# Gated recurrence and binarized FFN: half of chunk 10's gates ahead of the loop, the recurrence step ahead of up group 0, and chunk 14's low part ahead of a shift and an addition

## The chip, the cores and the metric

The kernel runs on one core of a Trainium2 chip. The metric is the device time of one execution in microseconds; lower is better. Five engines work side by side, each through its own queue of instructions: PE (matrix products), DVE and ACT (elementwise work), POOL (elementwise work) and SP, which here only issues transfers.

## The reference

Two layers run over x of shape 2 x 4096 x 256 (batch, time, features). The first is a gated recurrence with a state of 64:

```python
u = x @ W_in + b_in
g = sigmoid(x @ W_gate + b_gate)
h_t = tanh(h_prev @ A + u_t @ Bm)
y_t = h_t @ C.T + u_t @ D.T
y_t = g_t * y_t + (1.0 - g_t) * x_t
r = ys @ W_out + b_out + x
x1 = layernorm(x + r)
```

The second is a feed-forward layer with a width of 1024, whose weights are their signs times the mean magnitude of each row:

```python
h = gelu(x1 @ bw1.T + b1)
out = layernorm(x1 + h @ bw2.T + b2)
```

All is float32.

## The kernel before, in words

**Recurrence.** Each sequence is cut into 64 segments that run side by side, so one step of the recurrence handles 2 x 64 columns. There are 64 steps, preceded by 48 warm-up steps from which the states at the segments' beginnings come: 112 in all. A step (`steps`, L156) is one matmul on PE (L157) and one tanh on ACT (L158), and it reads the tanh of the step before it. Function `step` (L673) puts one into the order if its inputs are there and steps are left; `emit` (L664) does the same by a count of PE's cost in the part ahead of the loop.

**Chunks.** The 64 time positions are handled as 16 chunks of 4 positions, 512 columns each. For one chunk the work is:

- gates: four matmuls (two halves `m`, two parts `k`) and a tanh for each half (`gates`, L300, written as a generator that yields after so many blocks of 128 columns)
- `mix` (L369) and `mix_end` (L384): C and D times state and input, then the gated sum on DVE
- `project` (L392): the product with W_out in blocks, then a sum on DVE
- `stats1`, `shift`, `norm`: the first layer norm; statistics on DVE, the power -0.5 on POOL (L265), the shift on DVE (L270), the application on ACT (L278)
- a transposed copy of the normalized block, split into a high part `xhi` on ACT and a low part `xlo` on DVE. For chunks 0, 1 and 15 `turn` (L425) does this through PE; for the others `blocks` (L444) transposes 32 x 32 squares on DVE and sends 16 small transfers through SP's queue into `xlo`, then `split_hi` (L461) copies `xlo` to `xhi` on ACT and `split_lo` (L466) subtracts on DVE
- `rest` (L472): b2 added on POOL
- `up` in four groups of eight matmuls (L486), each followed by two gelus (L496) and a cast (L505) on ACT; `low` (L508) subtracts the cast from the gelus on DVE
- `down` in four groups of 16 matmuls (L528)
- `add`, `stats`, `store`: the scaled sum, the second layer norm (shift and application in `store`, L559) and the transfer out

**Order.** The program order of each engine is written out by hand (`manual_schedule`, L697); no scheduler changes it. Ahead of the loop, the gates of chunks 0 to 9 are handed out by `parts` (L693) three blocks at a time between the steps. The loop over c (L777) then interleaves four chunks: up and down of chunk c, down groups 2 and 3 and the store of c - 1, the layer norm and split of c + 1, mix and project of c + 2, and two gate matmul pairs of chunks 10 to 15 from L814. In one iteration with 0 < c < 14 PE's order is: up 0 (L784), step, down 2 of c - 1, mix, up 1, step, down 3 of c - 1, gates, up 2, step, down 0, project, up 3, step, down 1. ACT's order beside it, from up 2 on, is: two gelus, cast, tanh of the step, `split_hi`, four applications of the store of c - 1 (L832), two gelus of up 3, cast, tanh of the step, four applications of `norm` of chunk c + 2, two gelus of up 0 of c + 1.

**Buffers.** The gates, the inputs' product and the up groups share three PSUM banks (`p_1`, L63); the step has one (L149). The transposed x has eight buffers (XTB), the gates nine (TGB).

Of the kernel before, what the change touches and what calls it, by code (L numbers as in the profile page):

```python
# [18 lines left out]
KD = DM // P  # L19
# [7 lines left out]
NC = L // SPC  # L27
TB = N // P
# [9 lines left out]
def gated_recurrence_then_binary_ffn(  # L38
# [16 lines left out]
    nc = tc.nc  # L55
# [68 lines left out]
    def u_of_chunks(*chunks):  # L124

        n = N * len(chunks) // 2
        parts = [(chunks[0], 0), (chunks[1], 0) if len(chunks) == 2 else (chunks[0], 1)]
        ps = p_1.tile([P, N], FP, tag="h", name=f"ps_u{chunks[0]}")
        for k in range(KD):
            for (c, i), r in zip(parts, (LOW, TOP)):  # L130
                nc.tensor.matmul(  # L131
                    ps[r, :n],
                    w_in[k],
                    x_tiles[c][:, k, bass.ts(i, n)],
                    start=k == 0,
                    stop=k == KD - 1,
                    skip_group_check=True,
                )
        for (c, i), r in zip(parts, (LOW, TOP)):
            to = u_of[:, bass.ds(c * SPC + i * n // W, n // W)].rearrange("p j b k -> p (j b k)")  # L140
            if r is TOP and c == FIRST:
                nc.scalar.activation(to, ps[r, :n], AF.Identity, bias=bin_c[r, :])
            else:
                nc.vector.tensor_scalar(to, ps[r, :n], bin_c[r, :], None, ALU.add)
        have_u.update(chunks)
        yield
# [144 lines left out]
    def later(what, *args):  # L291
        if waiting is None:
            what(*args)
        else:
            waiting.append((what, args))
            if len(waiting) > 1 and not held:
                what, args = waiting.pop(0)
                what(*args)

    def gates(chunks, size, x_of=lambda c: x_tiles[c.c]):  # L300

        room = size
        for c in chunks:
            xt_ = x_of(c)
            c.t = wk.tile([P, KD, N], FP, tag="tg", name=f"tg{c.nm}", bufs=TGB)
            for m in range(KD):
                ps = p_1.tile([P, N], FP, tag="h", name=f"ps_g{c.nm}_{m}")
                for k in range(KD):
                    i = 0
                    while i < TB:  # L310
                        n = min(room, TB - i)
                        cut = bass.ds(i * P, n * P)
                        nc.tensor.matmul(  # L313
                            ps[:, cut],
                            w_gate[:, k, bass.ts(m, P)],
                            xt_[:, k, cut],
                            start=k == 0 and i == 0,
                            stop=k == KD - 1,
                            skip_group_check=True,
                        )  # L320
                        i += n
                        room -= n
                        if k == KD - 1 and i == TB:
                            later(c.tanh, m, ps)
                        if room == 0:
                            room = size
                            yield

    class Chunk:

# [28 lines left out]
                nc.gpsimd.tensor_tensor(r[:, i, :], r[:, i, :], row, ALU.add)  # L359

        def gate(self):
            yield from gates([self], TB, lambda c: c.xt)

        def tanh(self, m, ps):
            nc.scalar.activation(
# [193 lines left out]
        def store(self, blocks=range(TB), engine=nc.vector, queue=nc.sync):  # L559

            cut = slice(blocks[0], blocks[-1] + 1)
            if engine is nc.scalar:
                self.st2.shift(blocks)
            self.st2.apply(blocks, engine)
            queue.dma_start(
                out=self.at(out, self.c)[:, cut, :], in_=self.x1[:, cut, :]
            )
            yield
# [69 lines left out]
    ch = [Chunk(c, f"{c}") for c in range(NC)]  # L638
# [8 lines left out]
    def ready():  # L647
        return done < len(plan) and plan[done] // SPC in have_u

    def next_steps():  # L650
        nonlocal done
        steps(plan[done])
        done += 1
        if done == WARM:
            first_states()
        for i in range(3):
            if done == WARM + (i + 1) * SPC:
                ch[i].load_h()
        if waiting and not held:
            for what, args in waiting:  # L660
                what(*args)
            waiting.clear()

    def emit(what, pieces, pace=5600):  # L664
        nonlocal since
        for _ in pieces:
            since += COST.get(what, 0)
            if since >= pace:
                since = min(since - pace, pace // 2)
                if ready():  # L670
                    next_steps()

    def step():  # L673
        if ready():
            next_steps()

    def do(i, what, *args, pace=5600):
        if not 0 <= i < len(ch):
            return
        if what == "load":  # L680
            need = WARM + (ch[i].c + 1) * SPC
            while done < need:
                next_steps()
            ch[i].load_u()
            ch[i].load_h()
        elif what in ("load_n", "load_x", "load_gate_x"):
            getattr(ch[i], what)()
        else:
            emit(what, getattr(ch[i], what)(*args), pace)

    early = gates([ch[i] for i in (4, 5, 6, 7, 0, 1, 2, 3, 8, 9)], 3)

    def parts(n, pace):  # L693
        emit("part", (next(early, None) for _ in range(n)), pace)

    ET = mybir.EngineType
    with tc.manual_schedule(engines={ET.PE, ET.Activation, ET.DVE, ET.Pool, ET.SP}):  # L697
# [39 lines left out]
        for i in range(4):  # L737
            ch[i].xt = x_tiles[i]
        ch[0].in_x = ch[1].in_x = True
        parts(1, 600)  # L740
        do(0, "mix", pace=850)
        do(0, "mix_end")
# [13 lines left out]
        do(0, "norm")  # L756
        do(1, "project", 1, pace=1700)
        do(1, "stats1")
        parts(1, 1700)
        while waiting:  # L760
            next_steps()
        waiting = None
# [4 lines left out]
        do(1, "norm", nc.vector)  # L767
        do(0, "rest")
        next(mixed)
        parts(2, 1700)  # L770
        for i in (4, 5):
            do(i, "load_x")
        end = len(ch) - 1
        parts_met = compare()
        since = -1 << 40
        late = gates(ch[10:], TB)
        for c in range(end):  # L777
            far = 0 < c < end - 1
            if far:
                do(c + 1, "shift")  # L780
                do(c + 1, "norm")
                do(c - 1, "low", 3)
                do(c + 1, "blocks")
            do(c, "up", 0)  # L784
            if c == end - 1:
                do(c - 1, "low", 3)
                do(c + 1, "shift")
                do(c + 1, "norm")
            step()
            do(c - 1, "down", 2)  # L790
            if c > 0:
                do(c + 2, "mix")
            do(c, "low", 0)
            mixed = ch[c + 2].mix_end() if 0 < c < end - 1 else iter(())
            next(mixed, None)
            if c == end - 1:
                assert done == len(plan), done
                next(parts_met)
                next(parts_met)
            do(c + 3, "load")  # L800
            do(c + 6, "load_x")
            if c % 2 == 0:
                do(10 + c // 2, "load_gate_x")
            do(c, "up", 1)
            step()
            do(c - 1, "down", 3)
            next(mixed, None)

            if c <= 12 or c == end - 1:
                do(c - 1, "add")  # L810
            if c <= 12:
                do(c - 1, "stats")
            if 1 <= c <= 12:
                emit("gate", (next(late, None) for _ in range(KD)))  # L814
            if not far:
                do(c + 1, "turn")
            do(c, "low", 1)
            if c == end - 2:
                do(c - 1, "add")
            if c > 12:  # L820
                do(c - 1, "stats")
            if c == end - 1:
                next(parts_met)
                next(parts_met)
            do(c + 1, "rest")
            do(c, "up", 2)
            step()
            if far:
                do(c + 1, "split_hi")
            do(c, "low", 2)  # L830
            if c < end - 1:
                do(c - 1, "store", range(TB), nc.scalar)  # L832
            do(c + 3, "load_n")
            do(c, "down", 0)
            do(c + 2, "project", 0)
            if c == end - 2:
                do(c + 1, "split_lo")
            do(c + 2, "project", 1)
            if far and c < end - 2:
                do(c + 1, "split_lo")  # L840
            do(c + 2, "stats1")
            do(c, "up", 3)
            if c == end - 1:
                do(c - 1, "store", range(TB), nc.scalar)
            step()
            do(c, "down", 1)
# [82 lines left out]
```

## Time and profile before

| what | value |
|---|---|
| median of 3 runs | 438.04 us (437.59 to 438.13) |
| the profiled execution's own time | 437.67 us |
| its span | 435.9 us |
| mean granted PE clock | 0.994 |
| PE busy | 425.5 us (98%) |
| DVE busy | 332.4 us (76%) |
| ACT busy | 286.0 us (66%) |
| POOL busy | 155.8 us (36%) |
| traffic | 51.34 MB, mean 118 GB/s |

The span is from the first instruction to the last of one profiled execution; what lies around it, 1.8 us here, is part of the time. A group's row in the profile gives source line, engine, operation, the tile written and those read, shapes and count, then busy time, the mean of one in ns, and the idle time of that engine just ahead of it with what ended it. A timeline row gives start and duration in us. A matmul instruction of float32 data shows as two records. Matmuls overlap each other in the records, so their pace is read from start to start.

### The profile page before, as it was taken

To read this page: it belongs to the slowest core of one execution; us is meant where nothing else is said; L and a number is where in the kernel's file an instruction comes from. 1 tells how busy PE (TensorE), PEld (TensorE's weight loads), DVE (VectorE), ACT (ScalarE), POOL (GpSimd) and SP (SyncE) were. 2 spreads that over 40 slices of the span, in tenths; PEclk is the share of its full clock that TensorE was granted. 3 is DMA by queue.
4 is the path that set the end of the run, shared out by engine and by line. 5 is a ranking of instruction groups with operands and counts; after the bars stand their busy time and mean duration, and the time that the engine had idled before them with its cause. 6 is when DMAs were issued, how large, how long until landed. Compare 5 with 4: busy or idle time off the path is not lost.

```text
span 435.9 us, 6818 instructions
## 1 busy us (share of the span) xinstructions
PE 425.5 (98%) x2402; PEld 344.3 (79%) x2402; DVE 332.4 (76%) x569; ACT 286.0 (66%) x480; POOL 155.8 (36%) x176
## 2 busy tenths in 40 slices
PE   8999999999999999999999999999999999999992
PEld 5665767788888879797979797978888888888982
DVE  0245937895979798888888897979797979797674
ACT  2443452486587776767677776777767585849881
POOL 1000050474143435253525443444343444533413
PEclk9999999999999999999999999999999999999997
DMA  8877713400251615152426242534233232311102
GB/s 297 300 282 261 269 36 128 163 2 0 44 174 44 217 46 178 38 186 80 144 66 192 76 144 69 166 102 124 91 107 109 58 111 60 111 36 50 48 2 102
DMA packets 31479, 51.34 MB, mean 118 GB/s; under 512 B 5328, under 2 KB 19664, under 8 KB 31440
## 3 DMA queue, kind: packets, MB, share of 16 engines
q1 hardware_dynamic: 30864, 50.48, 36.4%
q8 instruction: 21, 0.34, 0.3%
q10 hardware_dynamic: 576, 0.37, 0.3%
q14 instruction: 18, 0.15, 0.1%
HBM read 31.43 MB, written 8.39 MB: 91 GB/s over the span
## 4 chain that ended last, share of the span: by engine, by line
PE 89%; DVE 5%; ACT 2%; DMA 1%; issue 1%; POOL 1%; SPq 0%; POOLq 0%; DVEq 0%
PE ps_h L486 25%; PE ps_o L528 25%; PE ps_g L313 12%; PE ps_z L399 11%; PE ps_y L374 6%; PE ps_s L157 6%; PE ps_u L131 3%; DMA xt<-in_xT 1%; DVE hlo L512 1%; ACT xn L278 1%; POOL rs_b L265 1%; PE ps_t L430 1%; DVE bs_b L255 1%; DVE d L381 1%; ACT h L496 1%
## 5 line engine op out<-in xcount | busy, mean ns | idle before, releaser
L528 PE MATMUL ps_o<-sg,hhi 128*128 128x256 f32 x496 | 121.4, 286 | 0.0
L528 PE MATMUL ps_o<-sg,hlo 128*128 128x256 f32 x496 | 117.9, 279 | 0.1
L496 ACT ACTIVATE h<-ps_h,bias_c,al 128x512 f32<-128x512 f32 x128 | 95.5, 771 | 16.8 <-PE ps_h L486 13.0
L528 PEld LDWEIGHTS ps_o<-sg,hhi 128*128 128x128 f32 x496 | 93.5, 189 | 1.1 <-DVE o L544 0.3
L528 PEld LDWEIGHTS ps_o<-sg,hlo 128*128 128x128 f32 x496 | 93.5, 188 | 1.1 <-DVE hlo L512 0.3
L486 PE MATMUL ps_h<-xhi,sg 128*128 128x512 f32 x256 | 92.9, 444 | 0.3 <-ACT h L496 0.3
L359 POOL TENSOR_TENSOR xn<-xn,bo_r 128x256 f32<-128x256 f32 x64 | 54.7, 888 | 88.6 <-DMA xn<-in_x 78.4
L512 DVE TENSOR_TENSOR hlo<-h,hhi 128x1024 fp32r<-128x1024 f32 (+1 forms) x65 | 79.5, 1240 | 5.0 <-ACT hhi L505 5.0
L486 PE MATMUL ps_h<-xlo,sg 128*128 128x512 f32 x256 | 80.1, 394 | 0.2
L265 POOL TENSOR_TENSOR rs_b<-rs_b,neg_half 128x4 f32<-128x4 f32 (+1 forms) x17 | 28.1, 1655 | 115.1 <-DVE rs_b L264 105.0
L505 ACT CAST hhi<-h 128x1024 fp32r<-128x1024 f32 (+1 forms) x65 | 67.4, 1039 | 2.0
L313 PE MATMUL ps_g<-xt,w_gate 128*128 128x384 f32 (+3 forms) x208 | 66.2, 430 | 0.1
L486 PEld LDWEIGHTS ps_h<-xhi,sg 128*128 128x128 f32 x256 | 46.5, 189 | 18.9 <-issue 11.7
L158 ACT ACTIVATE st<-ps_s 64x128 f32<-64x128 f32 x112 | 30.0, 268 | 45.7 <-PE ps_s L157 45.3
L486 PEld LDWEIGHTS ps_h<-xlo,sg 128*128 128x128 f32 x256 | 48.0, 188 | 11.9 <-DVE xlo L440 0.7
L157 PEld LDWEIGHTS ps_s<-st,wab 128*128 128x128 f32 x224 | 38.5, 189 | 21.6 <-ACT st L158 9.7
L359 POOL TENSOR_TENSOR xn<-xn,b_r 128x256 f32<-128x256 f32 x64 | 52.9, 855 | 1.1 <-PE ps_t L430 1.1
L399 PE MATMUL ps_z<-w_out,tg 128*128 128x256 f32 x224 | 50.6, 379 | 0.0
L399 PEld LDWEIGHTS ps_z<-w_out,tg 128*128 128x128 f32 x224 | 41.4, 190 | 5.1
L157 PE MATMUL ps_s<-st,wab 128*128 128x128 f32 x224 | 43.8, 277 | 0.1
L278 ACT ACTIVATE xn<-xn,nm_a,rs_a 128x256 f32<-128x256 f32 x60 | 31.2, 591 | 14.4 <-DVE nm_a L270 14.3
L265 POOL TENSOR_TENSOR rs_a<-rs_a,neg_half 128x4 f32<-128x4 f32 x16 | 17.2, 1072 | 65.0 <-DVE rs_a L264 63.0
(79 smaller groups left out, 481.5 us busy)
## 6 DMA issues: line engine op xcount, KB each, us to landing
xt<-in_xT SPq DMA_DIRECT2D x35, 512.0 KB, 4.4
xn<-in_x SPq DMA_DIRECT2D x16, 512.0 KB, 3.4
out_y<-xn SPq DMA_DIRECT2D x15, 512.0 KB, 2.6
xlo<-xb SPq DMA_DIRECT2D x208, 32.0 KB, 1.9
hu<-st SPq DMA_DIRECT2D x32, 128.0 KB, 2.3
w1t<-in_w1T SPq DMA_DIRECT2D x2, 512.0 KB, 4.9
w1n<-in_w SPq DMA_DIRECT2D x2, 512.0 KB, 6.1
w2t<-in_w2T SPq DMA_DIRECT2D x2, 512.0 KB, 5.2
```

The source lines that it names most:

```text
L157: nc.tensor.matmul(p_h, ab, st[:, j].rearrange("p b k -> p (b k)"), start=True, stop=True)
L158: nc.scalar.activation(h_of[:, j + 1].rearrange("p b k -> p (b k)"), p_h[TOP, :], AF.Tanh)
L265: nc.gpsimd.tensor_tensor(rs, rs, neg_half[:, cut], ALU.pow)
L278: nc.scalar.activation(r, r, AF.Identity, bias=self.sh[:, i : i + 1], scale=rs)
L313: nc.tensor.matmul(ps[:, cut], w_gate[:, k, bass.ts(m, P)], xt_[:, k, cut], start=k == 0 and i == 0, stop=k == KD - 1, skip_group_check=True,)
L359: nc.gpsimd.tensor_tensor(r[:, i, :], r[:, i, :], row, ALU.add)
L399: nc.tensor.matmul(self.ps_z[:, i, :], self.y[:, k, bass.ts(i, P)], w_out[:, k, :], start=k == 0, stop=k == KD - 1,)
L486: nc.tensor.matmul(ps, sg1[:, k, bass.ts(j, P)], part[:, k, :], start=n == 0, stop=n == 2 * KD - 1,)
L496: nc.scalar.activation(to, ps.rearrange("p (a i c) -> p a i c", a=P // 32, c=32) if self.far else ps, AF.Gelu, bias=b1_c[:, j : j + 1], sc ...
L505: nc.scalar.copy(hi[:, part, :], h[:, part, :])
L512: nc.vector.tensor_sub(lo[:, i, :], h[:, i, :], hi[:, i, :].bitcast(FP))
L528: nc.tensor.matmul(ps[:, i, :], part[:, j % 2, bass.ts(tb, P)], sg2[:, j, :], start=j == 0 and part is self.h[j // 2][0] and first, stop=j ...
```

## The change

Four edits are made; the computation stays what it was.

- The gate generators for chunks 4 to 9 and 0 to 3 and for chunks 10 to 15 become one stream, whose piece size is 3 blocks ahead of the loop and 4 from the loop on. Ahead of the loop, `parts` takes one piece more ahead of chunk 0's turn and one more ahead of the loop: that is the first half of chunk 10's gates. Iteration 1 takes no gates any more. Chunk 10's x is loaded ahead of chunk 0's mix, not in iteration 0.
- For c > 0 the step that followed up group 0 comes ahead of it, right after down group 1 of the iteration before.
- In iteration 13 `split_lo` of chunk 14 is followed by the shift of chunk 12's store, which so far came ahead of it; the store's four applications and its transfer come after up group 3.
- In iteration 13 `rest` of chunk 14 comes after `stats1` of chunk 15, ahead of up group 3, no longer ahead of up group 2.

```diff
     def gates(chunks, size, x_of=lambda c: x_tiles[c.c]):
 
-        room = size
+        room = size[0]
         for c in chunks:
...
                         if room == 0:
-                            room = size
                             yield
+                            room = size[0]
...
-            yield from gates([self], TB, lambda c: c.xt)
+            yield from gates([self], [TB], lambda c: c.xt)
...
-            if engine is nc.scalar:
+            if engine is nc.scalar and not hasattr(self.st2, "sh"):
                 self.st2.shift(blocks)
...
-    early = gates([ch[i] for i in (4, 5, 6, 7, 0, 1, 2, 3, 8, 9)], 3)
+    size = [3]
+    stream = gates([ch[i] for i in (4, 5, 6, 7, 0, 1, 2, 3, 8, 9, *range(10, NC))], size)
 
     def parts(n, pace):
-        emit("part", (next(early, None) for _ in range(n)), pace)
+        emit("part", (next(stream) for _ in range(n)), pace)
...
         ch[0].in_x = ch[1].in_x = True
+        do(10, "load_gate_x")
         parts(1, 600)
...
-        parts(1, 1700)
+        parts(2, 1700)
         while waiting:
             next_steps()
...
-        parts(2, 1700)
+        parts(3, 1700)
...
-        late = gates(ch[10:], TB)
+        size[0] = TB
         for c in range(end):
...
+            if c > 0:
+                step()
             do(c, "up", 0)
...
-            step()
+            if c == 0:
+                step()
             do(c - 1, "down", 2)
...
-            if c % 2 == 0:
+            if c > 0 and c % 2 == 0:
                 do(10 + c // 2, "load_gate_x")
...
-            if 1 <= c <= 12:
-                emit("gate", (next(late, None) for _ in range(KD)))
+            if 2 <= c <= 12:
+                emit("gate", (next(stream) for _ in range(KD)))
...
-            do(c + 1, "rest")
+            if c != end - 2:
+                do(c + 1, "rest")
...
-            if c < end - 1:
+            if c < end - 2:
                 do(c - 1, "store", range(TB), nc.scalar)
...
                 do(c + 1, "split_lo")
+                ch[c - 1].st2.shift(range(TB))
...
             do(c + 2, "stats1")
+            if c == end - 2:
+                do(c + 1, "rest")
             do(c, "up", 3)
-            if c == end - 1:
+            if c >= end - 2:
                 do(c - 1, "store", range(TB), nc.scalar)
```

## The prediction

> **What bounds the kernel now.** I read the page's busy shares first, then the waits by total, then the chain of waits, then the timelines of PE and ACT around the places that the diff touches. The first line says that PE is the bound; the two lines from the table of waits are the longest that PE itself has in the whole span.
>
> ```profile
> PE 425.5 (98%) x2402; PEld 344.3 (79%) x2402; DVE 332.4 (76%) x569; ACT 286.0 (66%) x480; POOL 155.8 (36%) x176
> PE ps_s L154 <- POOL ones L107: 1.0, 1, 1.0
> PE ps_h L486 <- ACT h L496: 0.3, 1, 0.3
> ```
>
> Since a waiting matmul can be drawn as a long one, I checked starts against starts: 16 down matmuls take 1.83 us, 8 up matmuls 1.83 us, a recurrence step 0.22 us, four gate records 1.72 us, and one loop iteration 22.51 us (up group 0 at 215.76, then 238.27). That is the sum of its matmuls. The loop has almost nothing to give; it can only get worse. Lost time lies in three places: about 1.3 us between 83 and 91 us, 0.92 us at 391.85, and the start and end, which the diff leaves alone.
>
> Next, what a step needs. A step's matmul reads the tanh of the step before. This is ACT's timeline near the end of one iteration (start, duration):
>
> ```profile
> 230.83 0.26 ACT L158 ACTIVATE st<-ps_s 64x128 f32<-64x128 f32 x1
> 234.15 1.05 ACT L463 CAST xhi<-xlo 128x1024 fp32r<-128x1024 f32 x1 [3.06 <-DVE nm_b L270]
> 235.10 2.08 ACT L278 ACTIVATE xn<-xn,nm_b,rs_b 128x256 f32<-128x256 f32 x4
> 237.08 1.43 ACT L496 ACTIVATE h<-ps_h,bias_c,al 128x512 f32<-128x512 f32 x2
> 238.54 1.05 ACT L505 CAST hhi<-h 128x1024 fp32r<-128x1024 f32 x1
> 239.50 0.27 ACT L158 ACTIVATE st<-ps_s 64x128 f32<-64x128 f32 x1
> 240.12 2.08 ACT L278 ACTIVATE xn<-xn,nm_a,rs_a 128x256 f32<-128x256 f32 x4 [0.36 <-DVE nm_a L270]
> ```
>
> And PE's timeline over the same stretch:
>
> ```profile
> 236.22 0.38 PE L157 MATMUL ps_s<-st,wab 128*128 128x128 f32 x2
> 236.35 0.37 PE L528 MATMUL ps_o<-sg,hhi 128*128 128x256 f32 x1
> ...
> 238.15 0.28 PE L528 MATMUL ps_o<-sg,hlo 128*128 128x256 f32 x1
> 238.27 0.62 PE L486 MATMUL ps_h<-xhi,sg 128*128 128x512 f32 x2
> ```
>
> The step after up group 3 is multiplied at 236.22, but its tanh stands on ACT behind the copy xhi, four applies, two gelus and a cast, and ends at 239.77. PE is at up group 0 at 238.27. Today nobody cares, because the next step comes only after that group, at 240.10. The xhi copy is late because of the small transfers into xlo:
>
> ```profile
> ACT xhi L463 <- DMA xlo<-xb: 17.7, 7, 2.9
> ```
>
> What PE does when it meets such a tanh is seen once, ahead of chunk 0's turn: up group 1 would end at 90.52, and the step starts at 90.74, 0.06 after the tanh (90.42 + 0.26).
>
> ```profile
> 90.06 0.62 PE L486 MATMUL ps_h<-xlo,sg 128*128 128x512 f32 x2
> 90.74 0.49 PE L157 MATMUL ps_s<-st,wab 128*128 128x128 f32 x2
> ```
>
> **What the Trainium skill says.** "TensorE: Matmul & The Clock Gate", section "Step-by-step: what each phase is for": only weight loads are pulled ahead, matmuls stay in program order. The trace agrees: nothing overtook the step at 90.74. So work behind a waiting step waits too. The same page, "Back-to-back issue gap", gives N/2.4 + 2.5 ns warm, 216 ns for 512 columns; the up group's pitch here is 228 ns, so no faster matmul is hidden under these groups. "Perfetto Trace Analysis", section "Identifying the Most-Contended Engine", warns that matmul busy time says little on headroom, hence the start-to-start sums. "DMA: Bandwidth & Descriptors", section "Latency and other measured facts", puts a fixed cost of about 2 us on a transfer; the page here shows 1.9 us for xlo to land, after 16 issues on SP's queue at some 0.64 us each.
>
> **The change, part by part.**
>
> *Gates ahead of the loop.* Two more parts stand before the loop: chunk 10's first gate half, eight blocks in four pieces, 8 x 0.215 = 1.72 us of PE (before: two 512-column matmuls, the same streaming). One more part stands ahead of chunk 0's turn, one more ahead of its up group 0. Two stalls there are filled. The fourth normalized block ends at 83.88, and turn, begun at 83.25, took 1.28 instead of 0.80 us; with 0.65 us more ahead of it, it begins at 83.90 and loses perhaps 0.05. Up group 0 started near 86.05 and got its second xlo half late:
>
> ```profile
> 86.59 1.10 PE L486 MATMUL ps_h<-xlo,sg 128*128 128x512 f32 x2
> 87.52 0.63 PE L486 MATMUL ps_h<-xhi,sg 128*128 128x512 f32 x2
> ```
>
> That cost 0.55 us. In the new order it starts at 82.60 + 1.30 + 0.85 (turn) + 0.44 (mean of w2) + 1.30 (two parts) + 0.22 (step) + 0.64 = 87.35, with both xlo halves done near 87.3. It ends at 89.18 against 88.46: +0.72, of 1.72 us moved. 1.00 us is gained. The stall at 90.74 stays as it is. The extra tanh (0.69 us) falls where ACT idles. The transfer of chunk 10's x goes ahead of two hu loads on SP, which is idle from 63.68 to 67.25; at 4.4 us it lands by 69, needed at 85. The loads of x for chunks 5 and 6 now take buffers of chunks 0 and 1, free at 76.5 and 82.4; behind them hu and xn of chunk 3 slip to about 84, needed after 103. Nothing.
> In iteration 1 the 1.72 us of gates disappear from PE.
>
> *Step ahead of up group 0*, ten times (chunks 1 to 10). Its 0.22 us only changes places. The price is the new wait. The tanh ended after up group 0's old start by 0.18, 1.33, 1.17, 1.04, 0.84, 0.58, 1.50, 0.88, 1.29 and 0.40 us in the ten iterations; each wait would be that plus 0.06. Behind the waiting step stand the up group, down 2, mix and all the rest. But a wait also slackens the next: the tanh hangs on transfers that began with the project of the iteration before, which ends ahead of the wait. Two equations follow. With z the start of project and S of the step: next z = S + 15.16 (238.27 to 253.42, 215.76 to 230.91). S is the later of z + 7.35 and the tanh's end + 0.06. The tanh's end is the last iteration's norm + 15.1 to 16.5 us (to the xhi copy, by iteration) + 5.6. That norm is at its z + 9.2 to 9.6, or behind its own tanh. Lower bound of the wait: even with ACT free, a tanh ends 2.23 us after its up group (200.74 to 202.97) and the down takes 2.05, so 0.24.
>
> Carried through: iteration 0 ends with S at 103.23 + 0.72 + 0.24 = 104.19. Iteration 1's project is at 104.19 + 15.16 - 1.72 = 117.63, but its tanh hangs on the norm at 105.26: xhi at 122.17, tanh 127.78, so PE, ready at 124.98, waits 2.9 us. The missing gates are eaten whole and more: S is 2.11 us behind before's place. From there the waits alternate between 0.24 and about 0.7 to 1.2. S stands behind before's up group 0 by 0.96, 2.11, 2.35, 3.21, 3.46, 3.86, 5.01, 5.26, 6.36, 6.60 us. After chunk 10 no steps are left and PE runs at its old pace. Gain ahead of the loop is inside this sum: +6.6.
>
> *End.* In iteration 13 the chain of waits reads:
>
> ```profile
> 388.14 1.87 POOL rs_b L265
> 390.03 0.71 DVE nm_b L270
> 390.77 2.08 ACT xn L278 x4
> 392.85 0.68 ACT h L496
> 393.57 1.20 PE ps_h L486 x4
> ```
>
> The shift nm_b delays xlo on DVE (to 392.5) and the four applies delay the gelu of up group 3, whose PSUM bank up group 0 of chunk 14 needs: 0.92 us lost. After: xlo goes first (390.3 to 391.6, needed at 392.3), the gelus follow the xhi copy at 390.3, and the bank is free at 391.1. The applies slide behind the cast to 392.8 to 394.9, up group 0's gelus to 394.9, norm of chunk 15 to 397.4 to 399.5; its turn, now due at 399.2, may lose 0.1. rest of chunk 14 on POOL goes behind a pow, needed only after 410. Gain 0.8. If the turn waited for more, the gain would shrink to 0.4; it can't exceed 0.92.
>
> Sum for the profiled execution: 437.67 + 6.6 - 0.8 = 443.5; the median of the three timed runs lies 0.37 above that execution, so 443.8.
>
> **Rivals.** (1) The waits don't slacken: whatever PE loses the transfers lose too. Then 9.8 us of waits, + 0.72 - 0.8, iteration 1 swallowing its gates: 437.67 + 9.7, median 447.8. Against it: the transfers start from work done before the wait. (2) Only the lower bound: if the transfers come quicker when shifted, ten waits of 0.24, so 2.4 - 1.0 - 0.8 = +0.6, median 438.6, no measurable change. For it, the spread of 1.4 us in norm to xhi; against it, ACT's idle time ahead of xhi in every iteration. (3) Faster: the wait at the step is hidden. The two repaired stalls are worth 1.8 us, so it decides at a mean wait of 0.18 us per step; with none, 435.9, median 436.2. The place is the down group between two steps: it would have to last as long as gelu, cast and tanh, which this trace shows in no iteration, the smallest lateness being 0.18. (4) The end's repair does nothing: 0.8 more, inside the range.
>
> **Numbers.** The forecast with (4) gets 0.80, (1) 0.09, (2) 0.06, (3) 0.05. The range 441.0 to 446.0 holds the forecast with norm to xhi at its short end throughout (15.1: about 2.5 us less) and at its long end (about 2 us more). Within 0.2% is 0.9 us, about what a measurement here can tell: faster 0.05, within 0.05, slower 0.90.
>
> **What would show it.** PE's timeline should have a hole ahead of the step before each up group 0 of chunks 1 to 10, ended by ACT's L158, the largest (near 3 us) ahead of chunk 2's, the rest 0.2 to 1.2; iterations of about 23.0 to 23.1 us; the table of waits should list ps_s L157 <- ACT st L158 near the top for PE or its weight loads. Turn of chunk 0 near 0.85 us, its up group 0 at 1.85. No stall at up group 0 of chunk 14. Iterations staying at 22.5 us would prove me wrong.

## The result, and the profile after

| what | before | after |
|---|---|---|
| median | 438.04 us (437.59 to 438.13) | 444.19 us (442.58 to 445.17) |
| ratio to before, 95% interval | | 1.0139 (1.0123 to 1.0155) |
| profiled execution: time, span | 437.67, 435.9 us | 443.37, 441.5 us |
| PE busy | 425.5 us (98%) | 428.2 us (97%) |

The change costs 6.1 us. The busy shares say little of it: PE's falls by one point, although PE now stands still for 5.15 us ahead of its steps, as the starts of its matmuls show below.

The table of waits of after (total us, how many, longest) shows what is new. Before, no step waited on PE for a tanh long enough to be listed; now that is PE's longest wait, with ACT's wait for the small transfers into xlo still large behind it.

```profile
ACT xhi L463 <- DMA xlo<-xb: 22.3, 10, 5.0
PEld ps_s L157 <- ACT st L158: 15.8, 40, 2.0
PE ps_s L157 <- ACT st L158: 2.9, 4, 1.8
```

Four waits of 2.9 us in all are not the loss. The table lists only those that the profile can put down to the tanh and that last long enough. PE's timeline is needed for the rest. This is its worst place, ahead of chunk 2's up group 0, in after:

```profile
125.69 0.28 PE L528 MATMUL ps_o<-sg,hlo 128*128 128x256 f32 x1
127.77 0.49 PE L157 MATMUL ps_s<-st,wab 128*128 128x128 f32 x2 [1.80 <-ACT st L158]
128.01 0.71 PE L486 MATMUL ps_h<-xhi,sg 128*128 128x512 f32 x2
```

Matmuls of 256 columns follow each other at 0.11 us, so down 1 is through at 125.80 and the hole is 1.97 us. ACT's timeline of after says what the step waited for:

```profile
121.91 1.05 ACT L463 CAST xhi<-xlo 128x1024 fp32r<-128x1024 f32 x1 [3.33 <-DMA xlo<-xb]
123.05 2.08 ACT L278 ACTIVATE xn<-xn,nm_b,rs_b 128x256 f32<-128x256 f32 x4
125.04 1.42 ACT L496 ACTIVATE h<-ps_h,bias_c,al 128x512 f32<-128x512 f32 x2
126.50 1.04 ACT L505 CAST hhi<-h 128x1024 fp32r<-128x1024 f32 x1
127.45 0.27 ACT L158 ACTIVATE st<-ps_s 64x128 f32<-64x128 f32 x1
```

From the landing of xlo on ACT never idles until the tanh ends at 127.72, and PE starts the step 0.05 later. Read in the same way, the holes ahead of the ten moved steps are 0.24, 1.97, 0.27, 0.43, 0.27, 0.46, 0.70, 0.27, 0.27 and 0.27 us, 5.15 together. Each costs some 0.10 more: a step and the up group behind it take 2.17 us from start to start after a wait, against 0.22 + 1.83 without one.

The loop's loss builds up as follows (start of the moved step in after less start of up group 0 in before, in us; the traces already differ by 0.15 at chunk 0's project, 72.98 against 72.83):

| ahead of chunk | 1 | 2 | 3 | 4 | 5 | 6 | 7 | 8 | 9 | 10 |
|---|---|---|---|---|---|---|---|---|---|---|
| predicted | 0.96 | 2.11 | 2.35 | 3.21 | 3.46 | 3.86 | 5.01 | 5.26 | 6.36 | 6.60 |
| measured, 0.15 taken off | 1.48 | 1.89 | 2.27 | 2.78 | 3.17 | 3.70 | 4.52 | 4.92 | 5.27 | 5.66 |

After chunk 10 the distance stays (+5.73 to +5.76 raw at up group 0 of chunks 11 to 14). The repair at the end brings it to +4.87. Then the turn of chunk 15 loses 0.61 us of that. These lines are from the timelines of ACT, DVE and PE of after, in this order:

```profile
395.53 1.05 ACT L463 CAST xhi<-xlo 128x1024 fp32r<-128x1024 f32 x1 [5.03 <-DMA xlo<-xb]
```

```profile
396.61 1.23 DVE L467 TENSOR_TENSOR xlo<-xlo,xhi 128x1024 fp32r<-128x1024 f32 x1 [1.73 <-ACT xhi L463]
397.82 1.22 DVE L410 SCALAR_TENSOR_TENSOR xn<-xn,ps_z 128x1024 f32<-128x1024 f32 x1
```

```profile
404.97 0.72 PE L430 MATMUL ps_t<-ident,xn 128*128 128x128 f32 x3
405.85 0.76 PE L430 MATMUL ps_t<-ident,xn 128*128 128x128 f32 x5 [0.16 <-ACT xn L278]
406.37 0.71 PE L486 MATMUL ps_h<-xhi,sg 128*128 128x512 f32 x2
```

`split_lo` now stands ahead of chunk 15's sum (L410) on DVE. It waited 1.73 us for an xhi that the transfer had made late, so the sum, the statistics and the norm of chunk 15 came late too, and turn took 1.40 us instead of 0.79. The spans differ by 5.6 us.

### The profile page after: what moved, and what is told of

Its sections match the earlier page's. It is cut to its first block, busy times and chain, and to the rows that moved or that the text cites. A ratio compares the mean times of both kernels' runs of the same rounds, so it can differ in the third digit from the quotient of the medians.

```text
span 441.5 us, 6821 instructions
## 1 busy us (share of the span) xinstructions
PE 428.2 (97%) x2406; PEld 346.2 (78%) x2406; DVE 326.5 (74%) x569; ACT 286.3 (65%) x480; POOL 147.9 (33%) x176
## 4 chain that ended last, share of the span: by engine, by line
PE 63%; DVE 14%; ACT 10%; SPq 6%; issue 3%; POOL 1%; DMA 0%; POOLq 0%; DVEq 0%; ACTq 0%
PE ps_h L486 16%; PE ps_o L528 14%; PE ps_g L313 10%; SPq L455 6%; PE ps_z L399 6%; PE ps_y L374 5%; PE ps_s L157 5%; ACT xn L278 5%; PE ps_u L131 4%; DVE hlo L512 3%; ACT h L496 3%; ACT hhi L505 2%; DVE bs_b L255 2%; DVE o L544 1%; DVE xn L550 1%
## 5 line engine op out<-in xcount | busy, mean ns | idle before, releaser
L512 DVE TENSOR_TENSOR hlo<-h,hhi 128x1024 fp32r<-128x1024 f32 (+1 forms) x65 | 77.8, 1215 | 4.7 <-ACT hhi L505 4.6
L359 POOL TENSOR_TENSOR xn<-xn,bo_r 128x256 f32<-128x256 f32 x64 | 47.5, 776 | 83.6 <-DMA xn<-in_x 81.3
L158 ACT ACTIVATE st<-ps_s 64x128 f32<-64x128 f32 x112 | 30.0, 268 | 45.7 <-PE ps_s L157 45.3
L157 PEld LDWEIGHTS ps_s<-st,wab 128*128 128x128 f32 x224 | 37.6, 188 | 26.5 <-ACT st L158 15.8
L157 PE MATMUL ps_s<-st,wab 128*128 128x128 f32 x224 | 45.0, 282 | 3.6 <-ACT st L158 2.9
```

Source lines behind the costliest of these rows:

```text
L157: nc.tensor.matmul(p_h, ab, st[:, j].rearrange("p b k -> p (b k)"), start=True, stop=True)
L158: nc.scalar.activation(h_of[:, j + 1].rearrange("p b k -> p (b k)"), p_h[TOP, :], AF.Tanh)
L512: nc.vector.tensor_sub(lo[:, i, :], h[:, i, :], hi[:, i, :].bitcast(FP))
```

## The experiments

The diffs are against the kernel named. Ratios are to the kernel before, with their 95% intervals.

**One part at a time.** First the changed kernel with the step behind up group 0 again, so that the other edits stand alone:

```diff
-            if c > 0:
-                step()
             do(c, "up", 0)
...
-            if c == 0:
-                step()
+            step()
             do(c - 1, "down", 2)
```

> The changed kernel with the step put back behind up group 0; gates and end repair stay. If the waits at the moved step are the cause, all of the loss goes and what is left is the gain ahead of the loop (about 0.7 us by the trace after) and at the end (about 0.3): 437.1 us, 436.6 to 437.6, and no matmul of the steps after 95 us waits. If moving the gates or the end's order had cost time, it stays at 438 us or above.

437.06 us, 0.9981 (0.9972 to 0.9990): the other edits together are worth a small gain, and the moved step is the whole loss. Next the kernel before with only the moved step:

```diff
+            if c > 0:
+                step()
             do(c, "up", 0)
...
-            step()
+            if c == 0:
+                step()
             do(c - 1, "down", 2)
```

> The kernel before with the step ahead of up group 0 and nothing else. Waits that slacken each other, as predicted: about +5.5 us, so 443.5 us, 442 to 445, with a first wait near 0.24 and a second near 1.4 us. Waits that pass on in full (ten times the old lateness plus a restart): 448 us. If the removed gates of iteration 1 were what made the step wait: 440 us or less.

444.23 us, 1.0135 (1.0120 to 1.0151), that is +5.9 us. Its ten holes are 0.18, 0.71, 1.13, 0.27, 0.28, 0.53, 0.65, 0.27, 0.52 and 0.36 us. The rival in which all waits pass on in full (448) is out. Then the gates alone (after, with the step and the end as they were before; the place of `rest` and the test in `store`, which belong to the end, are put back too and left out here):

```diff
-            if c > 0:
-                step()
             do(c, "up", 0)
...
-            if c == 0:
-                step()
+            step()
...
-            if c < end - 2:
+            if c < end - 1:
                 do(c - 1, "store", range(TB), nc.scalar)
...
-                ch[c - 1].st2.shift(range(TB))
...
-            if c >= end - 2:
+            if c == end - 1:
                 do(c - 1, "store", range(TB), nc.scalar)
```

> The kernel before with the gates' move alone. By the prediction's sum 1.0 us is gained ahead of the loop: 437.0 us. By the trace after, where a step between the gates and the turn waits too, 0.6 to 0.7: 437.4 us. If iteration 1 without gates has its own waits, no gain: 438.0 us.

438.25 us, 1.0008 (1.0000 to 1.0017): no gain, a miss. PE stands 1.44 us behind before where the loop starts, 0.2 to 0.3 ahead once iteration 1 has no gates, and 0.64 behind after the step that follows chunk 2's up group 0. From start to start that step comes 0.77 us late (the table of waits lists 0.6 of it), and the restart adds 0.10. Iteration 1 without its gates is 1.72 us shorter on PE, but the layer norm, the transfers and ACT's queue are not. The tanh that hides elsewhere is late there even behind up group 0. And the end alone (before, with the end's edits; the move of `rest` is left out here):

```diff
-            if engine is nc.scalar:
+            if engine is nc.scalar and not hasattr(self.st2, "sh"):
                 self.st2.shift(blocks)
...
-            if c < end - 1:
+            if c < end - 2:
                 do(c - 1, "store", range(TB), nc.scalar)
...
                 do(c + 1, "split_lo")
+                ch[c - 1].st2.shift(range(TB))
...
-            if c == end - 1:
+            if c >= end - 2:
                 do(c - 1, "store", range(TB), nc.scalar)
```

> The kernel before with the end's order alone. By the prediction's sum 0.8 us are gained: 437.2 us. By the trace after, where up group 0 of chunk 14 gains 0.9 and the turn of chunk 15 loses 0.6: 437.7 us, and the same 0.6 us stall at the turn.

437.52 us, 0.9992 (0.9986 to 0.9999). In its trace up group 0 of chunk 14 gains 0.88 us and the turn loses 0.10 (`split_lo` waited 1.22 us for xhi). The time shows less of it than the trace. The three parts alone sum to about +0.35 + 5.9 - 0.35 = +5.9 us, against +6.1 for all. Of gates and end it isn't so clear: apart they sum to 0.0 (each within some 0.35), together they measured -0.8 (-1.2 to -0.4), and the intervals just meet. The traces show no gain from the gates in either kernel: at chunk 12 PE is 0.51 us behind before with the gates alone and 0.22 behind with gates and end. The gain comes at the end, 1.05 us there and 0.78 with the end alone. Why these parts differ from kernel to kernel stays open.

**What makes the tanh late.** Two things stand ahead of it in ACT's queue: the cast of up group 3, which sets the lower bound, and the applications of `store`, which with the late xhi make the larger holes. Each was taken from in front of it in the changed kernel, with the step still ahead of up group 0. First the tanh issued ahead of the cast; PE's order is unchanged (`between` is called in `up` ahead of the cast):

```diff
+                    if between:
+                        between()
                     for part in range(2) if apart else [slice(0, 2)]:
...
-            do(c, "up", 3)
+            do(c, "up", 3, False, step)
...
-            step()
             do(c, "down", 1)
```

> The changed kernel, PE's order untouched, but on ACT the tanh of the step behind up group 3 goes ahead of that group's cast instead of behind it: the tanh ends 1.05 us earlier. If the step waits because of what stands ahead of its tanh on ACT, the holes of 0.24 to 0.70 us vanish and the one of 1.97 ahead of chunk 2 shrinks to about 0.9; of 6.2 us of waits and restarts 2 to 2.5 are left: 440.3 us, 439.3 to 441.5. If the step's place on PE itself costs (a restart or a joint between groups), it stays at 443 us or above.

438.87 us, 1.0021 (1.0013 to 1.0029): five of the six us come back, more than the expected range allowed. Holes are left ahead of chunk 2 (0.94 us), chunk 3 (0.50) and once later (0.32); the others are some 0.01, so the lower bound is gone. Then the store's applications and its transfer behind the tanh, in every iteration:

```diff
-            if c < end - 2:
-                do(c - 1, "store", range(TB), nc.scalar)
-            do(c + 3, "load_n")
+            if 0 < c < end - 2:
+                ch[c - 1].st2.shift(range(TB))
...
-            if c >= end - 2:
-                do(c - 1, "store", range(TB), nc.scalar)
             step()
+            do(c - 1, "store", range(TB), nc.scalar)
+            do(c + 3, "load_n")
```

> The changed kernel, step ahead of up group 0, with the store's four applications behind the step's tanh of up group 3 in every iteration (the shift stays in its place, the load of x for chunk c + 3 follows the store). The tanh no longer waits 2.08 us for the applications, but gelus and cast still end 2.2 us behind up group 3, and down takes 2.05: holes of about 0.24 and restarts of 0.10 in all ten, 3.4 us of 6.2, so 441.4 us, 440.4 to 442.6. If the applications have no part in it: 444 us. If the norm, now behind the applications, makes the transfers late in its turn: 443 us or above.

441.16 us, 1.0070 (1.0056 to 1.0084), as expected. Here the opposite is left: eight of the ten holes are 0.23 or 0.24 us, the other two 0.30 and 0.39. So the causes can be told apart: the cast behind the gelus makes 0.24 us in every iteration, the applications with the late xhi make what lies above it. The third way is more cover on PE: the step between the two halves of up group 0.

```diff
+            halves = ch[c].up(0)
+            next(halves)
             if c > 0:
                 step()
-            do(c, "up", 0)
+            next(halves)
```

> The changed kernel with the moved step between the two halves of up group 0, so 0.92 us later on PE and still earlier than before the change. Waits by lateness: holes under 0.9 vanish, the one ahead of chunk 2 shrinks to about 1.05: 440.4 us, 439.4 to 441.5. If any place ahead of the group's end costs the same, 444 us; if the waits pass on in full, each later one stays above 0.3 and the time above 441.5 us.

438.27 us, 1.0006 (0.9998 to 1.0014). Four matmuls, 0.91 us, hide nearly all; only chunk 2's iteration is long (23.63 us from project to project), the next ones 22.65, 22.52 and 22.49. More came back than the expected range allowed (more on this below). It fits the holes of after one by one: 0.91 us is more than each of them but chunk 2's (the next largest is 0.70), and that one should shrink from 1.97 to 1.06; the long iteration is 1.12 over before's 22.51.

**A better version.** With the step behind up group 0 again, one wait was left, behind chunk 2's up group 0 (listed as 0.49 us, 0.66 from start to start). One try puts only iteration 1's applications and transfer behind the tanh:

```diff
+            if c == 1:
+                ch[0].st2.shift(range(TB))
-            if c < end - 2:
+            elif c < end - 2:
                 do(c - 1, "store", range(TB), nc.scalar)
...
             step()
+            if c == 1 or c >= end - 2:
+                do(c - 1, "store", range(TB), nc.scalar)
```

> The changed kernel with the step put back and, in iteration 1 alone, the four applications and the transfer of chunk 0's store behind the step's tanh of up group 3 (load of x for chunk 4 behind them). With the step back alone, iteration 1 without gates lost 0.77 us at the step behind chunk 2's up group 0. If that tanh is late because the applications stand ahead of it, the 0.77 us come back: 436.3 us, 435.8 to 436.9. If it is late because of the gates' missing time alone, 437.06 us as with the step back.

437.07 us, 0.9974 (0.9964 to 0.9984), a miss: chunk 2's wait is gone, but iterations 2 and 3 lose 0.24 and 0.43 us. PE, now earlier, meets the chain of norm and transfers later on; the loss moved. The other puts the tanh ahead of up 3's cast, as above, in all iterations:

```diff
             do(c, "up", 0)
...
+            step()
             do(c - 1, "down", 2)
...
-            do(c, "up", 3)
+            do(c, "up", 3, False, step)
...
-            step()
             do(c, "down", 1)
```

> Step back behind up group 0, gates' move and end repair kept, and the step's tanh ahead of up group 3's cast in every iteration. With the step back alone 0.77 us were lost at the step behind chunk 2's up group 0; moving one store's applications only pushed the loss into iterations 2 and 3. If all of it is lateness of that tanh, 1.05 us earlier in every iteration returns nearly all: 436.4 us, 435.9 to 436.9. If PE, ahead by the missing gates, then meets something else that is late (a PSUM bank behind the gelus, the low part), 437.0 us as before.

436.72 us, 0.9974 (0.9966 to 0.9982), the lowest median here, 1.1 us under before; from the two others with the step behind up group 0 (0.9981 and 0.9974) its interval doesn't separate it. Behind chunk 2's up group 0 its PE timeline shows no wait, the step following the group at its pitch (the next step, behind up group 1, waits 0.10 us), and ACT's shows the tanh in its new place:

```profile
126.77 0.62 PE L486 MATMUL ps_h<-xlo,sg 128*128 128x512 f32 x2
127.23 0.38 PE L157 MATMUL ps_s<-st,wab 128*128 128x128 f32 x2
```

```profile
126.69 0.25 ACT L158 ACTIVATE st<-ps_s 64x128 f32<-64x128 f32 x1
126.85 1.03 ACT L507 CAST hhi<-h 128x1024 fp32r<-128x1024 f32 x1
```

**The turn of chunk 15, and a hole's second price.** To get the 0.6 us of the turn back, chunk 15's sum went ahead of `split_lo` in the changed kernel:

```diff
             do(c + 2, "project", 0)
+            do(c + 2, "project", 1)
             if c == end - 2:
                 do(c + 1, "split_lo")
                 ch[c - 1].st2.shift(range(TB))
-            do(c + 2, "project", 1)
```

> The changed kernel with chunk 15's sum of x and projection ahead of chunk 14's split_lo on DVE, where DVE stood idle for 1.7 us. In the trace after, the turn of chunk 15 lost 0.6 us to a norm that hangs on this sum. If so, the norm starts 1.2 us earlier relative to the project, turn takes 0.8 again and 0.6 us are gained: 443.6 us against 444.2, and the turn's time in the trace shows it. If the norm waits for ACT's applications instead, turn keeps its 1.4 us.

444.46 us, 1.0166 (1.0152 to 1.0180). In the trace the turn did shrink to 0.79 us, yet the time is no better. The view by windows (us; then for PE, weight loads, DVE, ACT and POOL the busy time with its count; then the granted clock, DMA's share and GB/s) shows one reason right behind chunk 2's hole, 2.28 us long in this execution:

```profile
128.00:131.00 3.00, 3.00 (x10) 2.38 (x11) 1.66 (x3) 2.47 (x6) 0.30 (x1) 0.61 0.54 175
128.00:128.60 0.60, 0.60 (x4) 0.56 (x5) 0.27 (x2) 0.07 (x1) 0.30 (x1) 1.00 0.00 0
128.70:132.00 3.30, 3.30 (x11) 2.63 (x10) 2.17 (x2) 3.14 (x7) 0.57 (x1) 0.50 0.49 159
132.10:135.00 2.90, 2.90 (x19) 2.18 (x18) 0.00 (x0) 1.33 (x2) 2.17 (x4) 1.00 0.15 34
```

The hole ends at 127.94. The clock granted to PE was still 1.00 up to 128.60, then 0.50 for about 3.4 us, then 1.00 again. Ten matmul records ran in the first 3 us, in which after has 20, and up group 0 took 3.16 us instead of 1.93. Half the clock for 3.4 us costs some 1.7 us, an estimate from these windows. In the profiled execution of after (hole 1.97) the clock stays at 1.00:

```profile
128.00:131.00 3.00, 3.00 (x20) 2.66 (x19) 1.51 (x3) 2.33 (x6) 0.44 (x1) 1.00 0.53 175
```

So a new theory: in part of the executions the hole costs its length and then a slow stretch. The mean clock of the executions supports it; a fall like this one, over some 440 us, lowers the mean by 0.004. With the long hole (the changed kernel and the one with the sum first, 11 executions) the mean is 0.989 to 0.992 in six, 0.993 to 0.996 in the rest. The 32 executions of two kernels without it that ran on the same chip as the one with the sum first (the kernel before, and the tanh ahead of the cast with the step behind up group 0) are all at 0.993 or more. Holes of about 1 us leave no such mark: with the tanh first (0.94) and with the step between the halves (1.05) all 35 executions are at 0.993 or more. The price in time agrees roughly: the six with the lower mean have a median of 445.05 us, the other five 443.5, although the profiled execution above is the fastest of its five (443.66). This is also a part of why those two experiments came out below their ranges, since both sums began at the median of after, 0.8 us above its profiled execution, in which the clock didn't fall.

The remedy tried was to fill the hole with eight products of ones, which nothing reads, into the bank that up group 0 then overwrites; the step waits for the same tanh. Once in the changed kernel and once in the one with the sum first:

```diff
+        def filled(ps):
+            for _ in range(8):
+                nc.tensor.matmul(ps[:, :P], ones, ones, start=True, stop=True)
+            step()
...
-            if c > 0:
+            if c > 0 and c != 2:
                 step()
-            do(c, "up", 0)
+            do(c, "up", 0, False, filled if c == 2 else None)
```

> The changed kernel with eight products of ones (128x128) on PE between chunk 1's down group 1 and the step ahead of chunk 2's up group 0: at some 0.22 us each they fill about 1.8 us of the hole there; nothing else changes. The step still waits for the same tanh, so the profiled path stays as it is. If the hole lets the clock fall in some executions and this makes the upper group of times (444.9 and above), the times gather near the lower group: median 443.2, none above 444.3. If the two groups have another cause, the median stays at 444.2 and times above 444.8 remain.

> The same filling in the kernel in which chunk 15's sum goes ahead of chunk 14's split_lo. If the fall of the clock had hidden the 0.6 us that this wins at the turn of chunk 15, the median is now 442.6, 0.6 below the kernel with the filling alone. If the sum's place is worth nothing, it equals the kernel with the filling alone.

441.79 us (441.53 to 442.90), 1.0091 (1.0074 to 1.0108), and 441.75 us (441.18 to 442.32), 1.0085 (1.0069 to 1.0101), 2.4 and 2.7 us under the same kernels with the hole open, and no mean clock under 0.993. Both expectations were too high, by 1.4 and 0.85 us. PE's timeline of the first shows that the path is the same:

```profile
125.46 1.95 PE L784 MATMUL ps_h<-ones 128*128 128x128 f32 x16
127.42 0.49 PE L157 MATMUL ps_s<-st,wab 128*128 128x128 f32 x2
```

The eight products follow each other at 0.22 us; the step then still waits for its tanh and starts 1.96 us after down 1, as in after.

How much of the 2.4 and 2.7 us is the filling's isn't shown. The filled kernels ran on another chip than the kernel with the sum first, and no kernel with the open hole ran there. Their transfers were quicker in iterations where the programs are the same. These are SP's 16 issues into xlo for chunk 3 (start, duration of all 16), first in after, then in the filled kernel:

```profile
132.10 10.92 SPq L455 DMA_DIRECT2D xlo<-xb  x16
```

```profile
131.74 10.30 SPq L455 DMA_DIRECT2D xlo<-xb  x16
```

For chunks 3 to 6 they take 10.30 to 10.32 us in both filled traces, 10.64 to 11.55 in the twelve others. Whether that is the chip's doing or the filling's isn't shown. The profiled execution of after, whose clock didn't fall, is 1.6 us slower than the filled one's, and none of that lies at the filled hole: by the starts of PE's groups 0.38 lies ahead of it, before the loop, 0.62 in the holes ahead of chunks 6 and 7 (0.46 and 0.70, 0.27 each in the filled one) and 0.58 at the turn. About 0.8 us is left that the filling may have saved by keeping the clock up: that is how far the median of after lies above its profiled execution, against 0.05 in the filled kernel.

The sum ahead of `split_lo` is worth nothing that the time shows between the two filled kernels (441.75 against 441.79), where the turn took 0.79 and 0.82 us. The loss at the turn wasn't one execution's accident, though. In the nine profiles with `split_lo` ahead of the sum the turn took 0.79 to 1.48 us, and four of them lose over 0.1 (the step between the halves 0.95, the tanh first 1.15, after 1.40, the store behind the tanh 1.48); with the sum first it took 0.79 both times.

## Why the prediction was right, and where its steps were off

The predicted 443.8 us stands against 444.19, and 443.5 for a profiled execution against 443.37. The mechanism is the one named. That the total is so close is in part luck: the loop was forecast 0.9 us too dear, the gain at the end 0.5 too large and the median's distance from the profiled execution 0.45 too small, and these cancel.

- **The wait at the step: right.** ACT's L158 ends the holes, the one ahead of chunk 2 is the largest, the iterations became longer (22.85 to 23.33 us from project to project behind chunk 2's, 23.0 to 23.1 forecast), and the moved step alone gives +5.9 us, with +6.6 forecast for the loop.
- **The lower bound of 0.24: right.** Five holes of after are 0.27, one 0.24. Its cause, the cast between gelu and tanh, was shown by taking it out.
- **"From there the waits alternate between 0.24 and about 0.7 to 1.2": too large.** They were 0.27 to 0.70. The term that was mis-sized is the way from the norm to the xhi copy, "15.1 to 16.5 us", taken over from before iteration by iteration. In after it stayed within 0.25 us of before's in eleven of 13 chunks, but it was 15.25 instead of 15.89 us for chunk 9 and 15.98 instead of 16.91 for chunk 2. The difference is in the issuing of the transfers on SP's queue: the 16 issues took 10.30 us instead of 10.94 for chunk 9, 11.20 instead of 12.11 for chunk 2. So the 1.10 forecast ahead of chunk 9 became the lower bound. The issues and the copy for chunk 9, in before (norm at 263.06) and then in after (norm at 267.44):

```profile
266.48 10.94 SPq L455 DMA_DIRECT2D xlo<-xb  x16
278.95 1.05 ACT L463 CAST xhi<-xlo 128x1024 fp32r<-128x1024 f32 x1 [2.85 <-DVE nm_b L270]
```

```profile
270.87 10.30 SPq L455 DMA_DIRECT2D xlo<-xb  x16
282.69 1.05 ACT L463 CAST xhi<-xlo 128x1024 fp32r<-128x1024 f32 x1 [1.44 <-DMA xlo<-xb]
```

- Ahead of chunks 4 and 7 the forecast's 0.86 and 1.15 became 0.43 and 0.70: the way was some 0.2 us shorter there, and PE came later by the restart of 0.10 us behind each hole, which wasn't in the sum. In the kernel with the moved step alone the larger hole stands ahead of chunk 3, where the way took 16.91 us against 16.19 in before; so part of it changes from trace to trace.
- From chunk 8 on the lower bound alone is left. The ten restarts together gave about 1 us of the missing back. The loop cost 5.7 instead of 6.6.
- **"1.00 us is gained" ahead of the loop: 0.66,** the 0.22 us of one more step set aside. The order changes more than the three parts: one step more is issued there, between two gate parts. The prediction counted as many steps as before. PE's timeline of after, with the step that came in:

```profile
82.75 1.46 PE L313 MATMUL ps_g<-xt,w_gate 128*128 128x384 f32 x4
84.24 0.49 PE L157 MATMUL ps_s<-st,wab 128*128 128x128 f32 x2
84.57 1.04 PE L430 MATMUL ps_t<-ident,xn 128*128 128x128 f32 x8
```

- That step waited about 0.2 us for its tanh behind chunk 0's norm on ACT and had a restart of 0.1 behind it, which is nearly all of the missing. The stall ahead of the turn is gone (turn 0.87 us) and so is that of up group 0; the one after up group 1 stayed, 0.31 us, as forecast.
- **"The missing gates are eaten whole": right.** The tanh ahead of chunk 2 was forecast to end at 127.78 and ended at 127.72. That it fits so well is luck: its norm came at 105.93 instead of 105.26, and the way to the copy was 0.93 shorter. The hole was 1.97 instead of 2.9 because PE came 0.8 later, through the smaller gain, the restart and the 0.15 between the traces. The gates alone gained nothing for the same reason.
- **"Gain 0.8" at the end: 0.88, then 0.61 given back at the turn** ("may lose 0.1") in the profiled execution of after. With the end alone it was 0.88 and 0.10. The chain into the turn, over xlo, sum and norm, is in the experiments; "may lose 0.1" was right for the end alone and too small for the changed kernel.
- **The median as the execution + 0.37: too small.** The median lies 0.8 above the profiled execution. A fall of the clock in part of the executions was no term of the prediction.
- **Rivals.** Waits passing on in full: out. The lower bound alone: true of the last three chunks in after, not of the whole. The hidden wait: it was said that down 1 would have to outlast gelu, cast and tanh; with the cast behind the tanh the step ahead of up group 0 comes to 1.0021, with half a group more of cover to 1.0006. The moved step gave no gain even where its waits were nearly hidden. The end's repair doing nothing: out, up group 0 of chunk 14 gained 0.88.

## What to carry to other kernels

A step of a recurrence on a full engine costs nothing only while the work between two steps outlasts the other engine's whole queue up to the result. List that queue, and move the small result ahead of the large cast before moving the consumer. Work moved out of a dense iteration pays only if the other chains of that iteration get shorter with it; else it comes back as a wait. A hole on PE is not always priced by its length alone: look at the granted clock behind it, and at the mean clock of every execution. And compare kernels that wait for transfers on one chip: the filled ones, measured on a chip of their own, had quicker transfers in most of the loop, and their gain can't be told apart from that.

## What the runs showed of the hardware

- A hole of 2.28 us on PE was followed, 0.7 us behind its end, by about 3.4 us at a granted clock of 0.50. The Trainium skill, "TensorE: Matmul & The Clock Gate", section "HAM oscillation — how this bites in real kernels", gives as the rule that there be no PE-idle gaps over some 3.4 us; here a shorter one was enough in one execution, and one of 1.97 wasn't in another. The measurement decides: about 2 us can be enough. With a hole of about 2 us six of 11 executions have a mean clock of 0.992 or less; with holes of 0.94 and 1.05 us none of 35 has.
- Eight products of ones of 128 columns took 1.78 us, 0.22 each from start to start.
- After a wait, a step and the up group behind it take 0.10 us more than without, at a granted clock of 1.00.
- SP's 16 issues of the small transfers into xlo took from 10.30 to 12.11 us in one execution of before and from 10.30 to 11.36 in one of after.
